# A scan kernel on one Trainium2 core: the product with C in two halves, each behind a scan of other columns

## The chip, the core and the metric

The kernel runs on one core of a Trainium2 chip. The metric is the device time of one execution in microseconds (us); the time of the kernel before is the median of three runs. The engines are named as in the profile: PE (matrix products), DVE (vector), ACT (activations), POOL (general elementwise), SP (which issues most DMAs). SBUF is the on-chip memory; PSUM is the small memory that PE writes its results to.

## The reference

Two layers on an image `x` of shape 4 x 512 x 64 x 64, both with a residual. The first cuts the 512 channels in four chunks of 128 and runs a Mamba block on each; the second is a linear attention. The heart of the first layer, and of the time, is a recurrence over 4096 positions for 256 inner channels and 16 states:

```python
def step(h, inp):
    dt_t, B_t, C_t, x_t = inp
    dA = jnp.exp(dt_t[:, :, None] * A)
    h = dA * h + (dt_t * x_t)[:, :, None] * B_t[:, None, :]
    y = jnp.einsum('bds,bs->bd', h, C_t)
    return (h, y)
...
y = ys.transpose(1, 0, 2) + xc * D_param
y = y * jax.nn.silu(z)
return jnp.einsum('bld,od->blo', y, out_proj_w)
```

Around it stand a group norm, a layer norm, the input and output projections, a second layer norm and a projection; then the attention layer with its own group norm. The change concerns the line `y = einsum(h, C_t)`: the product of every state with C, and the sum over states.

## The kernel before

**Tiling.** The positions are cut in 8 tiles of 512. A *step* is one batch, one tile and one of the four chunks: 4 x 8 x 4 = 128 steps. In a step the 256 inner channels (2 halves) times 16 states make 32 rows of 128 partitions: a partition holds one of 32 channels with one of 4 states. These rows are taken in *groups* of four scans; 8 groups make a step, 1024 groups the loop. The code counts in *slots* of two scans: 16 slots a step, 2048 in all; `jj` is 0 for a group's first slot and 1 for its second.

**A group.** For each scan ACT computes `dA` (`decay`, L713) into one of three PSUM buffers, three scans ahead. POOL computes `bx` for two scans at once (`drive`, L721), two slots ahead, into one of three buffers. DVE runs `tensor_tensor_scan` (L739) into `h[:, j, :]`, one quarter of the tile `h` (128 x 4 x 512); `h` has two buffers. After the fourth scan the whole of `h` is multiplied by C: POOL takes the last 128 of the 512 positions (L750, with C in SBUF, behind a copy of the last column to the state `st`, L749), DVE the first 384 (L754, `CUT` is 384), with C in PSUM: `c_all`, one buffer, written by PE (`c_row`) out of the step's row of C.

**The sum over states.** `fold_states` (L757) runs one scan into the next group: PE writes the next group's `c_all` (which has to wait until the product has read the last one), at a half's first group it starts the accumulator `y` with D times x (`diagonal`), and then adds the group's `h` into `y` by eight matmuls with `fold`. The first scan of the group after the next overwrites this `h`, so it waits for these.

**The order of the work.** The order on each engine is that of the program (a manual schedule). `slot` issues the two scans with their `decay`, then the products, then calls `after`, which hands out everything else by slot number: convolution and projections of the step after next on PE (`pc`, `pz`, `pd`), softplus of the next step at slot 3 with its table loads on ACT (`time_steps`, L620), silu at slot 10 (L1044), the copy of `y` out of PSUM at slots 0 and 8 (`take_y`, L774), the gate and the output projection of the step before, layer norms, and the attention of the batch before in the gaps (`pq`, `pk`, `pr`). PE, ACT, POOL and DVE each take their instructions strictly in this order: one that waits holds up all behind it on its engine.

In this document a group's *place* is its number in its step, 0 to 7; place p covers slots 2p and 2p + 1.

Of the kernel before, what the change touches and what calls it, by code (L numbers as in the profile page):

```python
# [11 lines left out]
ALU = mybir.AluOpType  # L12
# [12 lines left out]
def kernel(  # L25
# [24 lines left out]
    nc = tc.nc  # L50
# [7 lines left out]
    CUT = T - T // 4  # L58
# [3 lines left out]
    NJ = P // BLK  # L62
# [58 lines left out]
    def mm(out_, lhsT, rhs, abreast=1, **how):  # L121

        work["mm"] += (0.25 if rhs.dtype == BF16 else 1.0) * rhs.shape[-1] / T / abreast
        nc.tensor.matmul(out_, lhsT, rhs, **how)  # L124
# [3 lines left out]
    def diagonal(out_, w, rhs):  # L128

        for k in range(P // BLK):  # L130
            r = slice(k * BLK, (k + 1) * BLK)
            mm(out_[r, :], w[r, :], rhs[r, :], abreast=P // BLK, start=True, stop=False)
# [242 lines left out]
    def bc(v, n):  # L375
        return v.unsqueeze(1).to_broadcast([P, n, v.shape[-1]])
# [296 lines left out]
    JJ = NJ // 2  # L673
    SLOTS = NH * NQ * JJ
    AWAY = (3, 10)

    def place(g):

        n, r = divmod(g, SLOTS)
        e, r = divmod(r, NQ * JJ)  # L680
        return n, e, *divmod(r, JJ)

    b_all, c_all, c_sb, dAs, bxs, hs, ys = {}, {}, {}, {}, {}, {}, {}
# [8 lines left out]
    def b_row(g):  # L692
        n, e, q, _ = place(g)
        b_all[g // JJ] = wk.tile([P, T], F32, tag="b_all", name=f"b_all_{g}", bufs=3)
        for_states(b_all[g // JJ], fs[n]["b_rows"], q)

    def c_tail(g):
        n, e, q, _ = place(g)
        c_sb[g // JJ] = wk.tile([P, T - CUT], F32, tag="c_sb", name=f"c_sb_{g}", bufs=2)
        for_states(c_sb[g // JJ], fs[n]["c_rows"], q)  # L700

    def c_row(g):
        n, e, q, _ = place(g)
        got = ps_c.tile([P, CUT], F32, tag="c", name=f"c_all_{g}")
        mm(got, sel[:, q, :], fs[n]["parts"], start=True, stop=True)
        c_all[g // JJ] = got

    def decay(k):

        n, e, q, jj = place(k // 2)  # L710
        j = jj * 2 + k % 2
        dAs[k] = ps_d.tile([P, T], F32, tag="dA", name=f"dA_{k}")
        nc.scalar.activation(  # L713
            dAs[k], fs[n]["d_all", e][:, 0, j, :], AF.Exp, scale=a_t[:, e, j, q : q + 1]
        )

    def drive(g):

        n, e, q, jj = place(g)
        bxs[g] = wk.tile([P, 2, T], F32, tag="bx", name=f"bx_{g}", bufs=3)  # L720
        nc.gpsimd.tensor_tensor(  # L721
            bxs[g], fs[n]["d_all", e][:, 1, jj * 2 : jj * 2 + 2, :], bc(b_all[g // JJ], 2), ALU.mult
        )

    def slot(g, last, after):
        n, e, q, jj = place(g)
        b, t, c = steps[n]
        if g + 2 < last:
            drive(g + 2)
        if jj == 0:  # L730
            if g + 3 * JJ < last:
                b_row(g + 3 * JJ)
            hs[g // JJ] = wk.tile([P, NJ, T], F32, tag="h", name=f"h_{g}", bufs=2)
        elif g + 1 < last:
            c_tail(g + 1)
        h = hs[g // JJ]
        for i in range(2):
            j = jj * 2 + i
            nc.vector.tensor_tensor_scan(  # L739
                h[:, j, :], dAs.pop(2 * g + i), bxs[g][:, i, :],  # L740
                0.0 if t == 0 else st[:, c, e, q, j : j + 1], ALU.mult, ALU.add,
            )
            if 2 * g + i + LEAD < 2 * last:
                decay(2 * g + i + LEAD)
            if i == 0 and jj == 0 and g:
                fold_states(g - 1, last)
        del bxs[g]
        if jj == JJ - 1:
            nc.gpsimd.tensor_copy(st[:, c, e, q, :], h[:, :, T - 1])  # L749
            nc.gpsimd.tensor_tensor(  # L750
                h[:, :, CUT:], h[:, :, CUT:], bc(c_sb.pop(g // JJ), NJ), ALU.mult
            )
            own = h[:, :, :CUT]
            nc.vector.tensor_tensor(own, own, bc(c_all.pop(g // JJ), NJ), ALU.mult)  # L754
        after()

    def fold_states(g, last):  # L757

        n, e, q, _ = place(g)
        if g + 1 < last:  # L760
            c_row(g + 1)
        if q == 0:
            ys[n, e] = ps_y.tile([P, T], F32, tag="y", name=f"y_{n}_{e}")
            diagonal(ys[n, e], dg[:, e, :], fs[n]["xz"][:, 0, e, :])
        h = hs.pop(g // JJ)
        for j in range(NJ):
            mm(
                ys[n, e][j * BLK : (j + 1) * BLK, :], fold, h[:, j, :],
                start=False, stop=(q == NQ - 1), abreast=NJ,
            )  # L770
# [232 lines left out]
    N = len(steps)  # L1003
# [86 lines left out]
    with tc.manual_schedule():  # L1090
        credit, seen, mix, held[0], held_x[0] = 0.0, work["mm"], iter(()), 0, 0
        for n, (b, t, c) in enumerate(steps):
# [10 lines left out]
            for s in range(SLOTS):  # L1103
                def after():
# [62 lines left out]
                    seen = work["mm"]  # L1167

                slot(n * SLOTS + s, N * SLOTS, after)
            fs[n - 1].clear() if n else None  # L1170
        fold_states(N * SLOTS - 1, N * SLOTS)
        now[0] = None
        for _, what in due:
# [61 lines left out]
```

## Time and profile before

| what | value |
|---|---|
| median of three runs | 8033.95 us (8033.66 to 8039.26) |
| the profiled execution | 8026.47 us, of it the span shown in the profile 8024.7 us |
| loop, from the first product to the last | about 128 to 7558 us |
| end of the attention, after the loop | about 465 us |
| DVE's scans | 4096, mean 1.20 us with a constant start value (512 of them), 1.27 us otherwise |
| DVE's product with C | 1024, mean 1.755 us |
| POOL's product with C | 1024, mean 1.272 us |
| POOL's `bx` | 2048, mean 2.367 us |
| ACT's `dA` | 4096, mean 0.687 us |

Every time in the profile is from one profiled execution. A group's row gives the number of instructions, their busy time, the mean of one, and the idle time of the engine just before them with what ended it. Busy shares are means over the whole span, the start and the end of the attention included; the time of a change to the loop is read from the loop. Instructions of DVE may overlap a little at their ends, so that the sum of their durations is more than the time they take.

### The profile page before, as it was taken

Reading aid. Unit: us, or ns where it says so; the run is one execution under the profiler, and the core shown is the slowest. Engines: PE = TensorE matmul, PEld = TensorE weight load, DVE = VectorE, ACT = ScalarE, POOL = GpSimd, SP = SyncE. Lnnn points to the kernel's source line nnn. Section 1 sums busy time; section 2 is a strip of 40 time slices with the busy share of each in tenths; the row PEclk is TensorE's granted clock in tenths of the full one; section 3 lists DMA queues with packets and bytes.
Section 4 is the critical chain, followed back from the end, with each engine's and each line's share of the span. In section 5 each row is a group of like instructions: output and inputs, shape, how many; then the busy total and the mean of one; then the engine's idle time right before and its main releaser. Section 6 shows DMA issues by size and latency. Waiting matters only on the chain.

```text
span 8024.7 us, 91633 instructions
## 1 busy us (share of the span) xinstructions
PE 6503.6 (81%) x24880; PEld 2132.3 (27%) x24880; DVE 7050.9 (88%) x5766; ACT 5545.6 (69%) x8321; POOL 6886.8 (86%) x4597
## 2 busy tenths in 40 slices
PE   5676777677788888888788888888788888888599
PEld 1121211121223222322222222322122232322144
DVE  5999999999999999989999999999999999998600
ACT  4667777777777777777777777777777777776421
POOL 4999999999999899889999989899999989889600
PEclk7888888887899999999899999999899999999799
DMA  5666666666666666676666656677666666677402
GB/s 157 165 166 162 149 148 158 156 158 158 172 164 167 151 163 155 172 192 169 171 159 169 174 151 159 160 182 189 158 164 158 157 154 157 156 186 185 116 32 89
DMA packets 829192, 1265.93 MB, mean 158 GB/s; under 512 B 183912, under 2 KB 317560, under 8 KB 816384
## 3 DMA queue, kind: packets, MB, share of 16 engines
q1 hardware_dynamic: 804736, 1222.32, 59.9%
q0 software_dynamic: 16896, 33.56, 2.4%
q10 hardware_dynamic: 7040, 4.20, 0.2%
q8 instruction: 195, 3.19, 0.2%
q14 instruction: 325, 2.66, 0.1%
HBM read 1052.78 MB, written 206.57 MB: 157 GB/s over the span
## 4 chain that ended last, share of the span: by engine, by line
PE 29%; DVE 27%; ACT 22%; issue 8%; DMA 6%; POOL 3%; SPq 2%; DVEq 0%; POOLq 0%; ACTq 0%
DVE h L739 24%; ACT dA L713 9%; PE pc L124 8%; PE pq L124 5%; PE y L124 4%; DMA d_all<-d_rows 3%; PE po L124 3%; PE pp L124 3%; PE pr L124 3%; ACT xz L1044 2%; POOL bx L721 2%; SPq L688 2%; ACT L1145 1%; ACT L1044 1%; ACT L1123 1%
## 5 line engine op out<-in xcount | busy, mean ns | idle before, releaser
L721 POOL TENSOR_TENSOR bx<-d_all,b_all 128x1024 f32<-128x1024 f32 x2048 | 4827.4, 2367 | 283.6 <-DVE h L739 268.0
L739 DVE TENSOR_TENSOR_SCAN h<-dA,st,bx 128x512 f32<-128x512 f32 x3584 | 4330.9, 1265 | 207.7 <-ACT dA L713 196.3
L713 ACT ACTIVATE dA<-d_all,a_t 128x512 f32<-128x512 f32 x4096 | 2756.8, 687 | 1539.7 <-DVE h L739 1506.1
L754 DVE TENSOR_TENSOR h<-h,c_all 128x1536 f32<-128x1536 f32 x1024 | 1796.9, 1755 | 189.8 <-PE c_all L124 88.9
L750 POOL TENSOR_TENSOR h<-h,c_sb 128x512 f32<-128x512 f32 x1024 | 1302.2, 1272 | 153.5 <-DMA c_sb<-c_rows 56.1
L124 PE MATMUL y<-h,fold 128*32 128x512 f32 x8192 | 1251.1, 686 | 124.3 <-POOL h L750 119.7
L124 PE MATMUL pc<-xn,w_cv 128*128 128x512 f32 x2048 | 1107.0, 677 | 255.8 <-ACT dt L620 156.8
L124 PE MATMUL c_all<-parts,sel 128*128 128x384 bf16 x1024 | 359.5, 351 | 875.2 <-DVE h L754 873.6
L124 PE MATMUL pq<-w_qk,xa 128*128 128x512 f32 x2048 | 968.8, 606 | 2.2 <-ACT xa L367 2.2
L739 DVE TENSOR_TENSOR_SCAN h<-dA,bx 128x512 f32<-128x512 f32 x512 | 587.6, 1204 | 68.6 <-ACT dA L713 67.8
L124 PEld LDWEIGHTS pc<-xn,w_cv 128*128 128x128 f32 x2048 | 405.4, 209 | 899.6 <-issue 424.1
L124 PEld LDWEIGHTS pq<-w_qk,xa 128*128 128x128 f32 x2048 | 400.1, 197 | 494.5 <-issue 478.7
L124 PEld LDWEIGHTS y<-h,fold 128*32 128x32 f32 x8192 | 169.4, 113 | 1349.5 <-POOL h L750 866.1
L124 PE MATMUL pr<-xb,m 128*128 128x512 f32 x1024 | 488.9, 616 | 15.9 <-DMA xb<-x 11.9
L124 PE MATMUL pp<-xn,w_pr 128*128 128x512 f32 x1024 | 477.4, 597 | 6.0 <-DVE xn L414 6.0
L828 ACT ACTIVATE kq<-pq 128x512 f32<-128x512 f32 x256 | 150.4, 587 | 270.5 <-PE pq L124 269.9
L777 POOL TENSOR_TENSOR xz<-xz 128x512 f32<-128x512 f32 x256 | 325.0, 1270 | 11.7 <-ACT xz L774 7.8
L124 PE MATMUL y<-xz,dg 32*32 32x512 f32 x2048 | 333.4, 726 | 0.0
L628 POOL TENSOR_TENSOR dt<-dt,xz 128x1024 f32<-128x1024 f32 x128 | 302.0, 2359 | 22.6 <-ACT dt L620 22.6
L124 PE MATMUL pd<-xz,w_xp 128*128 128x512 f32 x512 | 314.4, 745 | 7.8 <-ACT xz L1044 7.8
L749 POOL COPY st<-h 128x4 f32<-128x4 f32 x1024 | 210.2, 205 | 108.3 <-DVE h L739 91.2
L124 PE MATMUL pz<-xn,w_z 128*128 128x512 f32 x512 | 273.9, 627 | 8.8 <-DVE kq L835 3.3
(179 smaller groups left out, 5991.5 us busy)
## 6 DMA issues: line engine op xcount, KB each, us to landing
d_all<-d_rows SPq DMA_DIRECT2D x2048, 256.0 KB, 6.5
b_all<-b_rows SPq DMA_DIRECT2D x4096, 64.0 KB, 2.1
d_rows<-dt SPq DMA_DIRECT2D x256, 512.0 KB, 3.7
c_sb<-c_rows SPq DMA_DIRECT2D x4096, 16.0 KB, 1.8
xs<-in_x_dram SPq DMA_DIRECT2D x32, 1024.0 KB, 5.8
xn<-in_x_dram SPq DMA_DIRECT2D x32, 1024.0 KB, 5.8
xr<-in_x_dram POOLq DMA_DIRECT2D x32, 1024.0 KB, 10.5
x<-xr SPq DMA_DIRECT2D x32, 1024.0 KB, 4.2
```

Of the source, the lines that this page charges most:

```text
L124: nc.tensor.matmul(out_, lhsT, rhs, **how)
L628: nc.gpsimd.tensor_tensor(f["both"][:, 1], f["both"][:, 0], f["xz"][:, 0], ALU.mult)
L688: nc.sync.dma_start(dst[k * BLK : (k + 1) * BLK, :], rows_[q * KS + k, :].partition_broadcast(BLK))
L713: nc.scalar.activation(dAs[k], fs[n]["d_all", e][:, 0, j, :], AF.Exp, scale=a_t[:, e, j, q : q + 1])
L721: nc.gpsimd.tensor_tensor(bxs[g], fs[n]["d_all", e][:, 1, jj * 2 : jj * 2 + 2, :], bc(b_all[g // JJ], 2), ALU.mult)
L739: nc.vector.tensor_tensor_scan(h[:, j, :], dAs.pop(2 * g + i), bxs[g][:, i, :], 0.0 if t == 0 else st[:, c, e, q, j : j + 1], ALU.mult, AL ...
L749: nc.gpsimd.tensor_copy(st[:, c, e, q, :], h[:, :, T - 1])
L750: nc.gpsimd.tensor_tensor(h[:, :, CUT:], h[:, :, CUT:], bc(c_sb.pop(g // JJ), NJ), ALU.mult)
L754: nc.vector.tensor_tensor(own, own, bc(c_all.pop(g // JJ), NJ), ALU.mult)
L777: nc.gpsimd.tensor_tensor(f["xz"][:, 1, e, :], f["xz"][:, 1, e, :], f["xz"][:, 0, e, :], ALU.mult)
L828: nc.scalar.activation(qk[i], pq, AF.Relu)
L1044: nc.scalar.activation(fs[n]["xz"], fs[n]["xz"], AF.Silu)
```

## The change

The product with C on DVE is cut in two halves of two scans each. The first half, columns of the scans `j` = 0 and 1, stands where the whole product stood, behind the group's fourth scan. The second half, `j` = 2 and 3, is issued in the next group's first slot, behind its first scan and ahead of `fold_states`. In the order of DVE:

```
before: scan 0, scan 1, scan 2, scan 3, product(0..3) | scan 0, scan 1, ...
after:  scan 0, scan 1, scan 2, scan 3, product(0, 1) | scan 0, product(2, 3), scan 1, ...
```

`c_all` is no longer taken out of its table by the product, since both halves read it. The last group's second half follows the loop. The order on PE, ACT, POOL and SP is the same as before. On PE the wait for the product with C, which stood on the matmul that writes the next `c_all`, stands on the weight load ahead of it, and waits for the second half.

```diff
             if 2 * g + i + LEAD < 2 * last:
                 decay(2 * g + i + LEAD)
             if i == 0 and jj == 0 and g:
+                product(g - 1, 1)
                 fold_states(g - 1, last)
         del bxs[g]
         if jj == JJ - 1:
...
             nc.gpsimd.tensor_tensor(
                 h[:, :, CUT:], h[:, :, CUT:], bc(c_sb.pop(g // JJ), NJ), ALU.mult
             )
-            own = h[:, :, :CUT]
-            nc.vector.tensor_tensor(own, own, bc(c_all.pop(g // JJ), NJ), ALU.mult)
+            product(g, 0)
         after()
+
+    def product(g, jj):
+
+        own = hs[g // JJ][:, jj * 2 : jj * 2 + 2, :CUT]
+        nc.vector.tensor_tensor(own, own, bc(c_all[g // JJ], 2), ALU.mult)
...
             fs[n - 1].clear() if n else None
+        product(N * SLOTS - 1, 1)
         fold_states(N * SLOTS - 1, N * SLOTS)
```

## The prediction

> **What bounds the kernel now.** I read the busy shares first, then the same engines by stretch, then who waits for whom, then DVE's own timeline. Shares of the whole span and the three costliest groups:
>
> ```profile
> PE 6503.6 (81%) x24880; PEld 2132.3 (27%) x24880; DVE 7050.9 (88%) x5766; ACT 5545.6 (69%) x8321; POOL 6886.8 (86%) x4597
> L721 POOL TENSOR_TENSOR bx<-d_all,b_all 128x1024 f32<-128x1024 f32 x2048 | 4827.4, 2367 | 283.6 <-DVE h L739 268.0
> L739 DVE TENSOR_TENSOR_SCAN h<-dA,st,bx 128x512 f32<-128x512 f32 x3584 | 4330.9, 1265 | 207.7 <-ACT dA L713 196.3
> L754 DVE TENSOR_TENSOR h<-h,c_all 128x1536 f32<-128x1536 f32 x1024 | 1796.9, 1755 | 189.8 <-PE c_all L124 88.9
> ```
>
> Busy time by stretch (us, then PE, PEld, DVE, ACT, POOL):
>
> ```profile
> 2000.00:4000.00 2000.00, 1683.56 (x6549) 554.32 (x6550) 1874.01 (x1523) 1470.78 (x2215) 1837.06 (x1225) 0.92 0.67 167
> 4000.00:6000.00 2000.00, 1687.79 (x6621) 559.97 (x6620) 1872.67 (x1526) 1473.21 (x2217) 1833.55 (x1223) 0.92 0.66 167
> 7560.00:8024.00 464.00, 429.27 (x1510) 195.57 (x1508) 22.99 (x72) 103.85 (x167) 4.14 (x4) 0.95 0.18 59
> ```
>
> Inside the loop DVE is busy 94% of the time and POOL 92%; PE 84%, ACT 74%. The last 464 us are PE's alone, and the change doesn't touch them. DVE's timeline (start, us, what; merged):
>
> ```profile
> 2562.20 1.76 DVE L754 TENSOR_TENSOR h<-h,c_all 128x1536 f32<-128x1536 f32 x1
> 2563.88 4.80 DVE L739 TENSOR_TENSOR_SCAN h<-dA,st,bx 128x512 f32<-128x512 f32 x4
> 2568.78 1.75 DVE L754 TENSOR_TENSOR h<-h,c_all 128x1536 f32<-128x1536 f32 x1
> ```
>
> Two things stand here. Four scans of 1.26 us take 4.80 and not 5.04: each begins about 0.084 before the one ahead ends, and so does the scan behind a product (2563.88, though 2562.20 + 1.76 = 2563.96). Only the product does not: the scans end at 2568.68 and it starts at 2568.78, because it reads what the last scan wrote and waits for it. From product to product: 6.58 us. Who waits (us in total, times, longest):
>
> ```profile
> DVE h L739 <- ACT dA L713: 264.1, 175, 46.7
> DVE h L754 <- PE c_all L124: 88.9, 76, 3.0
> DVE h L739 <- POOL bx L721: 4.3, 6, 1.7
> PE c_all L124 <- DVE h L754: 873.6, 356, 9.1
> PE pc L124 <- ACT dt L620: 156.8, 67, 4.1
> ```
>
> So 1024 x 6.58 = 6738 of the loop's 7430 us are the chain of scans and products, some 350 are DVE's norms and sums, and some 340 (after the first product) are waits for others. DVE sets the pace, in places relieved by ACT and PE.
>
> [...]
>
> **The change part by part.**
> 1. The wait. In the built program the first half waits for DVE's second scan of the group (two scans behind it), the second half for the fourth scan, with a half product and a scan between. So both waits are over before their turn comes. Scan-to-product falls from 1.365 (1.26 + 0.105) to 1.175 (1.26 - 0.084): -0.19 us a group.
> 2. One more instruction. Short products of the same kind are in the trace: L835, 256 elements, takes 0.399 behind a scan and 0.417 behind a product; the norm's subtraction (L428), 2048 elements, 2.262 behind a scan. Slope (2.262 - 0.399)/1792 = 1.04 ns an element, so 768 elements behind a scan: 0.399 + 512 x 0.00104 = 0.931; less the overlap, 0.847. Two of them 1.694, against 1.672 for the whole one. [...] A scan behind a product takes 1.277 and not 1.259, and there are now two of those: +0.018.
> 3. Sum of a group: 2 x 0.847 + 2 x 1.193 + 2 x 1.175 = 6.43 against 6.58: -0.15 us [...]. Over 1024 groups 154 us [...]: the ceiling.
> 4. What of it reaches the end. Sorting the trace by group, 268 of 1024 product-to-product intervals hold a wait of DVE for another engine. They cluster: in a step of 8 groups (place 0 to 7), place 6 (94 waits for ACT, behind silu and its table loads) and place 2 to 4 (73 for ACT, 69 for c_all). ACT's interludes start behind a scan and last as long as before, so there the wait grows by what the group saves: no gain. Before a late c_all the groups from place 2 on gain nothing either; with those, 358 groups are lost and 666 gain: 666 x 0.15 = 100 us.
> 5. PE is released later. With the fourth scan's start as zero, the product ended at 1.365 + 1.755 = 3.12; the second half ends at 1.175 + 0.847 + 1.193 + 0.931 = 4.15. c_all of the next group, its weight load (which now holds the wait, 0.10) and the y products come 1.03 to 1.13 us later, and c_all is needed 0.34 earlier (0.19 + 0.15). Where PE had waited for the product, 4.4 us were left between c_all and the next product; 3 remain. Where PE comes late (place 2 to 5), the release isn't what it waits for: between c_all of place 1 and of place 2 it stood idle for ACT's dt (softplus), median 2.0 us, and dt hangs on a scan, not on the product. That idle time hides the 1.1 us; it is shorter than 1.1 in 45 of 126 steps, and only some of these have a tight c_all behind them: sum of shortfalls 12 us. In the 65 steps with a c_all that comes within 0.2 us of its product, the 0.19 already won at place 1 is lost too: 12 us.
> 6. h has two buffers, and a group's first scan waits for the y products of two groups before. y ends 1.00 us behind c_all. Before, a product of 1.67 covered that; now a half of 0.85 does. Where c_all is late, that adds some 0.17 us: 95 times, 16 us. The 24 at place 5 (y behind another matmul, 1.99) are covered by ACT's wait at place 6.
> 7. ACT, POOL and SP keep their order, and all DMAs theirs. ACT reads y one us later, but reaches that copy only behind the next group's second scan. POOL's tail product (L750) touches other columns and waits for the same scan. In 6 steps of about 53.5 us POOL is busy from end to end: 6 x 1 us are not to be had.
> Sum: 100 - 12 - 12 - 16 - 6 = 54 us. On the profiled execution: span 8024.7 to 7971 (8026.5 with what lies around it to 7973). The median of the runs is 7.5 above that execution: 8034 to 7980.
>
> **The rivals.**
> - *The whole ceiling.* The waiters are themselves driven by scans; if ACT's and PE's waits shrink with the more even rhythm (the fourth scan's dA gets 0.85 us more cover), nearly all arrives: 8034 - 154 = 7880. Against it: the ACT interludes of about 4.5 us at place 6 don't shrink.
> - *Absorbed.* POOL, 92% busy, or PE takes over as the bound: about 8025, from 8015 to 8034. For it: POOL's load is 2% below DVE's. Against it: POOL's bx lead its scans by a median of 3 to 5 us, and DVE waited for them 4.3 us in all.
> - *PE's lag decides (slower).* Place: c_all and y behind the second half. If PE's late stretch in each step hangs on the release and not on dt, every step loses 1.1 us: 128 x 1.1 = 141, less 100 gained, plus the 34 of points 6, 7 and the lost 0.19: +75, 8109. The point from which it decides is PE's idle time before the step's first pc falling to nothing; if it holds in three quarters of the steps, it is +40: 8074.
> - *It doesn't do what it says.* Were the first half still held till the last scan, only the costs remained: +0.04 us a group and points 5 and 6, about 8100. The waits of the built program speak against it.
>
> **How the numbers follow.** Likeliest 0.52 (its own range 7945 to 8010), ceiling 0.15, absorbed 0.15, PE's lag 0.14, not as said 0.04. A measurement here tells 0.2% (16 us) from no change. Faster: 0.51 + 0.15 + a third of the absorbed, 0.71. Same: 0.11. Slower: 0.14 + 0.04, 0.18. The range for 8 in 10 goes down to 7905, [...] and up to 8045, which takes in the absorbed case and the mild end of PE's lag.
>
> **What would show it.** Right: gap between the fourth scan and the first half -0.08 us and not +0.10; halves of 0.93; undisturbed groups of 6.43; DVE's waits for ACT up by 10 to 30 us; PE's wait for DVE before c_all about as long as before, moved into the weight load. Wrong: halves over 1.0, first scans waiting for y in hundreds of places, PE's wait for dt gone and DVE's for c_all doubled.

## The result, and the profile after

| | median, us | runs | ratio to before, 95% interval |
|---|---|---|---|
| before | 8033.8 | 4, 8031.7 to 8039.3 | |
| after | 7992.2 | 4, 7985.9 to 7998.0 | 0.9947 (0.9930 to 0.9964) |
| after, once more with later experiments | 7994.2 | 5, 7986.1 to 7996.0 | 0.9943 (0.9931 to 0.9956) |

The change takes 42 us off (8033.8 - 7992.2), forecast were 54. The profiled execution went from 8026.5 to 7990.5, its span from 8024.7 to 7988.8. The page of the changed kernel, the rows of DVE's loop and of PE's `c_all`:

```profile
PE 6502.1 (81%) x24835; PEld 2128.4 (27%) x24880; DVE 7037.6 (88%) x6790; ACT 5528.9 (69%) x8321; POOL 6881.1 (86%) x4597
L739 DVE TENSOR_TENSOR_SCAN h<-dA,st,bx 128x512 f32<-128x512 f32 x3584 | 4411.6, 1266 | 265.7 <-ACT dA L713 199.8
L760 DVE TENSOR_TENSOR h<-h,c_all 128x768 f32<-128x768 f32 x2048 | 1897.2, 926 | 92.7 <-PE c_all L124 92.4
L124 PE MATMUL c_all<-parts,sel 128*128 128x384 bf16 x1024 | 369.4, 361 | 1073.3 <-DVE h L760 1071.8
```

A half takes 0.926 us. The idle time ahead of the product on DVE, 189.8 us before, is 92.7, and nearly all of that is now the wait for `c_all` (92.4): the 0.1 us that stood in front of each product is gone. The scans' busy time is larger (4411.6 us for 4330.9) though one takes as long as before (1.266 for 1.265): busy time counts an overlap within a group of the page once, and the scans now overlap halves where they overlapped each other. DVE's timeline of the changed kernel (start, us, what; equal neighbours merged):

```profile
2559.02 0.93 DVE L760 TENSOR_TENSOR h<-h,c_all 128x768 f32<-128x768 f32 x1
2559.86 1.27 DVE L739 TENSOR_TENSOR_SCAN h<-dA,st,bx 128x512 f32<-128x512 f32 x1
2561.06 0.93 DVE L760 TENSOR_TENSOR h<-h,c_all 128x768 f32<-128x768 f32 x1
2561.91 3.62 DVE L739 TENSOR_TENSOR_SCAN h<-dA,st,bx 128x512 f32<-128x512 f32 x3
2565.45 0.93 DVE L760 TENSOR_TENSOR h<-h,c_all 128x768 f32<-128x768 f32 x1
```

From first half to first half: 6.43 us, where a group took 6.58. The first half at 2565.45 begins before the scans end (2561.91 + 3.62 = 2565.53); in this stretch every instruction overlaps the one ahead. Who waits (us in total, times, longest):

```profile
DVE h L739 <- ACT dA L713: 268.0, 192, 46.7
DVE h L760 <- PE c_all L124: 92.4, 67, 2.6
DVE h L739 <- PE y L124: 36.6, 69, 1.2
DVE h L739 <- POOL bx L721: 25.6, 23, 4.0
PE c_all L124 <- DVE h L760: 1071.8, 430, 10.1
PE pc L124 <- ACT dt L620: 78.1, 53, 2.9
```

What is new: scans that wait for `y` (36.6 us, 3.1 before) and for `bx` (25.6, 4.3 before). PE waits longer for the product (873.6 before) and less for dt (156.8 before), as it would if the later release moves PE's idle time from one place to the other.

Sorted by place, the interval from one group's fourth scan to the next one's, mean in us (worked out from the traces; the interval ends at the place named):

| place | 0 | 1 | 2 | 3 | 4 | 5 | 6 | 7 |
|---|---|---|---|---|---|---|---|---|
| before | 6.70 | 6.60 | 8.52 | 6.93 | 7.18 | 7.60 | 7.86 | 6.71 |
| after | 6.58 | 6.47 | 8.56 | 6.88 | 7.35 | 7.50 | 7.85 | 6.62 |

Places 7, 0, 1 and 5 gain about 0.1 a group, place 3 half of that. Places 2 and 6 gain nothing, as forecast: there ACT's softplus (3.86 us with its two table loads of 1.28 us each) and silu (4.51 us with its two) stand ahead of `dA`, and DVE waits for `dA` 93.6 and 96.3 us, of 268.0 in all. Place 4 loses 0.17: there the waits for a late `c_all` (65 us in all, 50 before, the overlap lost by the wait counted in) and most of those for `bx` (17 us of 29) come together.

### The profile page after: what moved, and what is told of

The parts are those of the page before. It is cut to its first block, busy times and chain, and to the rows that moved or that the text cites. A ratio compares the mean times of both kernels' runs of the same rounds, so it can differ in the third digit from the quotient of the medians.

```text
span 7988.8 us, 92611 instructions
## 1 busy us (share of the span) xinstructions
PE 6502.1 (81%) x24835; PEld 2128.4 (27%) x24880; DVE 7037.6 (88%) x6790; ACT 5528.9 (69%) x8321; POOL 6881.1 (86%) x4597
## 4 chain that ended last, share of the span: by engine, by line
PE 30%; DVE 27%; ACT 17%; DMA 10%; issue 8%; SPq 4%; POOL 3%; DVEq 0%; POOLq 0%; ACTq 0%
DVE h L739 17%; DVE h L760 8%; PE pc L124 7%; ACT dA L713 7%; PE pq L124 5%; PE y L124 5%; DMA d_all<-d_rows 5%; SPq L688 3%; PE pp L124 3%; PE pr L124 2%; PE po L124 2%; POOL bx L721 2%; ACT xz L1049 2%; DMA c_sb<-c_rows 1%; SPq L639 1%
## 5 line engine op out<-in xcount | busy, mean ns | idle before, releaser
L739 DVE TENSOR_TENSOR_SCAN h<-dA,st,bx 128x512 f32<-128x512 f32 x3584 | 4411.6, 1266 | 265.7 <-ACT dA L713 199.8
L760 DVE TENSOR_TENSOR h<-h,c_all 128x768 f32<-128x768 f32 x2048 | 1897.2, 926 | 92.7 <-PE c_all L124 92.4
L124 PE MATMUL y<-h,fold 128*32 128x512 f32 x8192 | 1276.0, 699 | 84.9 <-POOL h L751 84.1
L124 PE MATMUL c_all<-parts,sel 128*128 128x384 bf16 x1024 | 369.4, 361 | 1073.3 <-DVE h L760 1071.8
L124 PE MATMUL pc<-xn,w_cv 128*128 128x512 f32 x2048 | 1084.9, 665 | 150.3 <-ACT dt L620 78.1
L124 PEld LDWEIGHTS <-sel 128*128 128x128 bf16 x1280 | 127.5, 100 | 1712.1 <-DVE h L760 1466.0
```

The costliest lines, as they stand in the source:

```text
L739: nc.vector.tensor_tensor_scan(h[:, j, :], dAs.pop(2 * g + i), bxs[g][:, i, :], 0.0 if t == 0 else st[:, c, e, q, j : j + 1], ALU.mult, AL ...
L760: nc.vector.tensor_tensor(own, own, bc(c_all[g // JJ], 2), ALU.mult)
```

## The experiments

The theory: each undisturbed group gains 0.15 us because the product no longer waits for the scan ahead; where another engine is late the gain is lost, and the later release of PE takes some more. The rivals: POOL or ACT absorb what DVE saves; the gain has another source than the wait. All ratios are to the kernel before on the same chip.

**Both halves behind the fourth scan** (the split without the move):

```diff
             if i == 0 and jj == 0 and g:
-                product(g - 1, 1)
                 fold_states(g - 1, last)
...
             product(g, 0)
+            product(g, 1)
```

> Both halves stand behind the fourth scan, the second half straight behind the first; nothing is moved past the next group's first scan. Theory (the 0.15 us of each undisturbed group comes from the wait that goes; what is lost on the way is the later release of PE, seen as first scans that wait for y and products that wait for c_all): an undisturbed group again takes 6.43 us (1.175 + 0.847 + 0.865 + 1.193 + 2 x 1.175), DVE's waits for y fall from 36.6 us to under 10, PE's release comes 0.15 us before that of the kernel before, and the time is 7930 to 7955. Rival (the rest of the gain is taken by POOL and by ACT's interludes, wherever the half stands): 7980 to 8000, as with the changed kernel. Rival (the distance of a scan is needed, an adjacent half still waits): groups of 6.6 us and 8030 or more.

Measured: 7972.8 us, ratio 0.9924 (0.9911 to 0.9938); an undisturbed group takes 6.43 us. DVE's waits in that kernel:

```profile
DVE h L739 <- ACT dA L713: 306.2, 195, 46.4
DVE h L760 <- PE c_all L124: 102.0, 82, 3.9
DVE h L739 <- POOL bx L721: 19.2, 23, 2.8
DVE h L739 <- PE y L124: 4.4, 15, 0.3
```

The waits for `y` are nearly gone, as expected, and the time is 19 us below the changed kernel's (7992.2 - 7972.8). It isn't as low as I put it: with `y` on time, DVE waits 38 us more for ACT and 10 more for `c_all` than in the changed kernel. So these four kinds of wait don't say where the 19 us lie: together they are 432 us here and 423 in the changed kernel. By place, it is place 4 that shrinks, from 7.35 to 7.21 us (18 us in 128 steps).

DVE's timeline of this kernel shows both halves starting without a gap:

```profile
2549.74 4.80 DVE L739 TENSOR_TENSOR_SCAN h<-dA,st,bx 128x512 f32<-128x512 f32 x4
2554.46 1.79 DVE L760 TENSOR_TENSOR h<-h,c_all 128x768 f32<-128x768 f32 x2
```

The halves start at 2554.46, before the scans end (2554.54), and overlap each other. The second half needs no scan between itself and what it reads; the first half is distance enough. So the split by itself brings the gain, and the kernel that also moves the second half past the next group's first scan is 19 us slower.

One thing beside the order differs. These runs had a granted PE clock of 0.894 to 0.896, those of the changed kernel 0.888 to 0.892, and among the runs of one kernel those at a higher clock tend to be shorter (two further down, at 0.892, took 7974 and 7977 us; one of the same kernel at 0.888 took 8004). Whether PE's order sets that clock, and how much of the 19 us goes with it, was not tested. The same holds for the two kernels below that move the whole product (0.896 to 0.899).

**The split with the wait kept**: as above, but the half that reads the third and fourth scan first.

```diff
-            product(g, 0)
             product(g, 1)
+            product(g, 0)
```

> Both halves behind the fourth scan, the half that reads the third and fourth scan first: the split alone, with the wait for the last scan kept. Theory: an undisturbed group takes 6.65 us (0.07 more than before: two halves of 0.87 net for one product of 1.67), 8060 to 8085. Rival (the gain came from shorter instructions or from the split, not from the wait): below 8020.

Measured: 8074.3 us, ratio 1.0049 (1.0035 to 1.0063). Its DVE timeline:

```profile
2557.72 4.80 DVE L739 TENSOR_TENSOR_SCAN h<-dA,st,bx 128x512 f32<-128x512 f32 x4
2562.63 1.82 DVE L760 TENSOR_TENSOR h<-h,c_all 128x768 f32<-128x768 f32 x2
2564.37 2.45 DVE L739 TENSOR_TENSOR_SCAN h<-dA,st,bx 128x512 f32<-128x512 f32 x2
```

The scans end at 2562.52 and the halves start at 2562.63: the gap of 0.1 us is back, and group to group takes 2564.37 - 2557.72 = 6.65 us. This kernel and the pair have the same instructions and differ in the order of two of them; 0.22 us a group (6.65 - 6.43) and 101 us in all (8074.3 - 7972.8) lie between. That settles the source: it is the wait for the scan ahead.

**The product whole, behind the next group's first scan** (the move without the split):

```diff
             if i == 0 and jj == 0 and g:
-                product(g - 1, 1)
+                product(g - 1)
...
-            product(g, 0)
...
-        own = hs[g // JJ][:, jj * 2 : jj * 2 + 2, :CUT]
-        nc.vector.tensor_tensor(own, own, bc(c_all[g // JJ], 2), ALU.mult)
+        own = hs[g // JJ][:, :, :CUT]
+        nc.vector.tensor_tensor(own, own, bc(c_all[g // JJ], NJ), ALU.mult)
```

> The product whole, one instruction, behind the next group's first scan: the wait goes without a split. Theory: an undisturbed group takes 6.36 us (0.22 less than before), but the first scan of a group now stands ahead of the product and needs the y products of two groups before, so that DVE's waits for PE y rise to 60 to 150 us; 7940 to 8000. Rival (POOL or ACT is the bound once DVE saves anything): 7985 to 8000 with more waits for dA and bx instead of y.

Measured: 7964.7 us, ratio 0.9911 (0.9897 to 0.9924); an undisturbed group takes 6.365 us. The waits that stand out:

```profile
DVE h L739 <- ACT dA L713: 225.3, 183, 46.7
DVE h L739 <- PE y L124: 84.5, 81, 3.7
DVE h L739 <- POOL bx L721: 84.2, 74, 4.6
```

One instruction less a group, and the wait hidden too; paid for with scans that wait for `y`, as expected, and with as much for `bx`, which I had left to the rival. Both are right in part; the time is in the theory's range, and 28 us below the changed kernel (7992.2 - 7964.7).

**The second half and the sum one scan later**:

```diff
-            if i == 0 and jj == 0 and g:
+            if i == 1 and jj == 0 and g:
                 product(g - 1, 1)
                 fold_states(g - 1, last)
```

> As the changed kernel, but the second half and the sum over states stand one scan later, behind the next group's second scan: PE's release another 1.2 us later, DVE's instructions the same. Theory (the later release is what costs): waits of DVE for c_all and y rise by 30 to 80 us together, 8015 to 8060. Rival (the release is hidden and POOL and ACT take the rest): within 0.2% of the changed kernel, 7976 to 8008.

Measured: 8094.9 us, ratio 1.0072 (1.0058 to 1.0086): slower than before, though an undisturbed group still takes 6.43 us. The waits of this kernel, DVE's first, then PE's, then ACT's:

```profile
DVE h L739 <- ACT dA L713: 339.3, 230, 46.6
DVE h L760 <- PE c_all L124: 60.7, 56, 3.1
DVE h L739 <- PE y L124: 57.9, 80, 1.4
PE pc L124 <- ACT dt L620: 41.8, 40, 1.7
ACT xz L779 <- PE y L124: 345.4, 241, 7.4
```

The direction is the theory's, the time is above its range, and the road is another: waits for `c_all` and `y` together fell (118.6 for 129.0). What rose is ACT's: its copy of `y` out of PSUM waits 345 us for PE, 127.4 in the changed kernel, and the `dA` behind it come late (339 for 268). By place, the interval at 2 grows to 8.90 us, at 6 to 8.16, at 7 to 6.97. PE's idle time ahead of `pc` falls again. So the later release is cheap for one scan and dear for two: in the changed kernel ACT reaches that copy behind the next group's second scan and waits for `y` hardly longer than before (127.4 us, 124.7 before). That the late copy is what delays the `dA` is read from the waits and not tested; and DVE's waits for ACT, `c_all`, `y` and `bx` together rose by 57 us, of the 109 between the two spans (8097.4 and 7988.8).

**y before D times x**: in a half's first group PE adds the group's `h` first.

```diff
         for j in range(NJ):
             mm(
                 ys[n, e][j * BLK : (j + 1) * BLK, :], fold, h[:, j, :],
-                start=False, stop=(q == NQ - 1), abreast=NJ,
+                start=(q == 0), stop=(q == NQ - 1), abreast=NJ,
             )
+        if q == 0:
+            diagonal(ys[n, e], dg[:, e, :], fs[n]["xz"][:, 0, e, :], False)
```

> As the changed kernel, but in a half's first group PE adds the group's h into y first and D times x (1.0 us) behind it, so that h is free 1.0 us sooner twice a step. Theory (the first scan at place 6 waits for y because that matmul stands ahead, and ACT's wait covers only part of it): DVE's waits for PE y fall from 36.6 us to 5 to 15, the time falls by 8 to 25 us: 7967 to 7984. Rival (ACT's wait at place 6 takes over in full): waits for dA rise by as much, 7986 to 7998.

Measured: 7990.0 us (7974 to 8004, 6 runs), ratio 0.9940 (0.9928 to 0.9951): the changed kernel's time. Its waits:

```profile
DVE h L739 <- ACT dA L713: 305.5, 194, 48.2
DVE h L739 <- PE y L124: 7.2, 36, 0.8
```

29 us of waits for `y` go, 38 of waits for `dA` come: at place 6, where 29.5 of the 36.6 us were, DVE now waits for ACT's silu instead (31 us more), so a wait removed there shows the one beneath. The median is in the rival's range too. But the runs lie far apart: the profiled one, at 7976.5, and one at 7974 are in the theory's range, the other four are not. A gain of some us is not excluded.

**POOL relieved**: POOL's product with C for two of the four scans only, on the changed kernel and on the kernel before.

```diff
             nc.gpsimd.tensor_tensor(
-                h[:, :, CUT:], h[:, :, CUT:], bc(c_sb.pop(g // JJ), NJ), ALU.mult
+                h[:, :2, CUT:], h[:, :2, CUT:], bc(c_sb.pop(g // JJ), 2), ALU.mult
             )
```

> As the changed kernel, but POOL's product with C is done for the first two of the four scans only (0.63 us less on POOL a group; the last 128 positions of the other two are left without C). Theory (POOL takes a small part of the gain): DVE's waits for bx fall from 25.6 us to near 0, 7955 to 7975. Rival (POOL is the bound that absorbed the gain): 7930 or less, towards the ceiling of 7880.

> The kernel before with the same cut of POOL's product (the last 128 positions of the third and fourth scan are left without C): what POOL costs there. Theory: 10 to 15 us less than before, 8018 to 8030, so that POOL took 10 to 20 us more from the changed kernel. Rival (POOL costs both the same): the changed kernel and this one fall by the same amount.

Measured: 7967.3 us on the changed kernel, ratio 0.9915 (0.9902 to 0.9928), 8040.4 on the one before, 1.0004 (0.9995 to 1.0012). Before, POOL costs nothing, not even the 10 us of my expectation; after, the relief is worth 25 to 27 us (7992.2 or 7994.2 less 7967.3). Three of DVE's waits in the relieved changed kernel:

```profile
DVE h L739 <- PE y L124: 20.4, 54, 1.2
DVE h L739 <- POOL h L751: 18.3, 22, 1.2
DVE h L739 <- POOL bx L721: 15.4, 10, 3.1
```

Waits for `bx` don't go to nothing (15.4 of 25.6 stay), against the theory. Those for `y` fall by 16 us, but those for POOL's own product with C rise by as much (18.3, 1.3 in the changed kernel), nearly all at place 6: one stands in for the other. The profiled run, at 7979.1, is the slowest of the four and only 11 us shorter than the profiled one of the changed kernel, so its waits can't show the whole 25 us. By place it is again place 4 that shrinks, from 7.35 to 7.22 us (17 us in 128 steps). The clock was 0.889 to 0.890, as in the changed kernel. So it is shown that POOL, which cost nothing before, takes a share once DVE is faster; by which wait is shown only in part. It isn't the bound that takes all, or the time had gone to 7930.

**Both together**: both halves behind the fourth scan, and POOL relieved in the same way.

> Both halves behind the fourth scan, and POOL's product with C done for the first two scans only (the last 128 positions of the other two are left without C). Theory (PE's later release and POOL each took their own part of the gain, 20 and 25 us): the two add up, 7940 to 7955. Rival (they are the same loss, seen once as a wait for y and once as one for bx): no better than the better of the two alone, 7963 to 7975.

Measured: 7954.4 us (7952 to 7965, 4 runs), ratio 0.9901 (0.9885 to 0.9916); the changed kernel beside it 7994.2 (the last row of the first table). For that one this was expected:

> The changed kernel once more, beside the next one on the same chip, as the base of comparison. Expected 7984 to 8000.

Alone, the two were worth 19 and 25 us; together 40 (7994.2 - 7954.4), 18 below the pair alone and 13 below the relief alone. They nearly add up: two losses, for the most part, and not one seen twice. There is no trace of this kernel. What would fit is a wait of the pair's: PE waits 239.9 us there for POOL's product with C ahead of `y`, where it waits 84.1 in the changed kernel and 29.2 in the relieved one.

**A faster order**: the whole product behind the next group's first scan, and PE does `y`, then the next `c_all`, then D times x.

```diff
-        if g + 1 < last:
-            c_row(g + 1)
         if q == 0:
             ys[n, e] = ps_y.tile([P, T], F32, tag="y", name=f"y_{n}_{e}")
-            diagonal(ys[n, e], dg[:, e, :], fs[n]["xz"][:, 0, e, :])
...
+        if g + 1 < last:
+            c_row(g + 1)
+        if q == 0:
+            diagonal(ys[n, e], dg[:, e, :], fs[n]["xz"][:, 0, e, :], False)
```

> The product whole behind the next group's first scan, and in the sum over states PE does y first, then the next c_all (which is now needed a scan later), then D times x. Theory (the waits for y are what is left of the moved product's gain): DVE's waits for y fall from 84.5 us to 20 to 50, 7920 to 7955, faster than both kernels and than both halves behind the fourth scan (7973). Rival (POOL is the next bound): waits for bx rise from 84 us to 110 or more and the time stays within 10 us of 7965.

Measured: 7949.0 us, ratio 0.9889 (0.9876 to 0.9902): faster than both kernels, and than the product moved alone (7964.7). The time is in the range I gave, but by luck, for its waits say that the reason is not the one I gave:

```profile
DVE h L739 <- ACT dA L713: 296.2, 203, 46.7
DVE h L739 <- PE y L124: 83.0, 74, 3.7
DVE h L739 <- POOL bx L721: 51.4, 48, 4.4
```

The waits for `y` stayed (83.0 for 84.5); those for `bx` fell (51.4 for 84.2) and those for `dA` rose (296.2 for 225.3). The rival, more waits for `bx`, is wrong as well. Why PE's order shortens the waits for POOL, and what the 16 us come from, was not tried and stays open.

## Why the prediction was right

The sum was 100 gained, 46 lost, 54 in all; 42 were measured. The gain was right in cause and size; that the losses come out so near is in part luck, since one term was too small and others too large.

- *The wait and the second instruction (points 1 to 3).* Right to the hundredth: gap -0.08, halves 0.926 (0.931 forecast), groups 6.43. The second half ends 4.14 us behind the fourth scan's start (4.15 forecast). The reversed pair shows that the wait is the source, and that the split alone costs 0.07 us a group.
- *What reaches the end (point 4).* 666 groups of 0.15 were to give 100 us. In the traces some 685 of 1023 intervals hold no wait in either kernel, and together they are some 99 us shorter (0.144 each). Places 2 and 6 gained nothing, as said. What shrank the 99 to some 37 in the loop lies in the other 340 intervals or so.
- *The later release and the two buffers (points 5 and 6).* 12 + 16 us were put down for them; putting the second half back behind the first is worth 19. The 16 were too many: first scans wait 36.6 us for `y`, but 29.5 of these at place 6, where waits for ACT take their place when they go, as forecast, and only 7 elsewhere. The idle time behind dt shrank (156.8 to 78.1), as it must if it covers the later release; that it covered most of it is argued, not shown.
- *POOL (point 7).* The term that was mis-sized most. I counted 6 us, from 6 steps in which POOL works from end to end; relieving it gives 25 to 27 in the changed kernel, 18 in the pair, and nothing in the kernel before. A reading at fault: that `bx` leads its scans by a median of 3 to 5 us. The low end of that lead is what counted here. In the kernel before it is shortest at places 3 and 4; at place 4's first scan the median is 4.0 us, yet a tenth of the leads are below about 1.4. In the changed kernel a tenth of them there are below 0.05, and 15.6 of the 25.6 us of waits for `bx` are at this place. These waits are only a part of what POOL takes. With 25 us in place of 6 the sum would have been 35, and with 19 in place of 12 + 16 as well, 44.
- *The slower rival* (PE's lag decides) didn't happen, but one scan later the kernel is slower than before, 8095. By its waits it goes another way than I wrote, over ACT's copy of `y`, and not over `c_all`.
- *The ceiling* (7880) was not reached: ACT's waits didn't shrink (268.0 us for 264.1). The low end of my range, 7905, was an estimate that no run shows.
- *The signs.* Two of those named for a right forecast did not come: DVE's waits for ACT rose by 4 us (264.1 to 268.0) and not by 10 to 30, and PE's wait for DVE before `c_all` rose by 198 (873.6 to 1071.8) and did not stay. The signs named for a wrong one did not come either: 69 waits for `y`, not hundreds; half of PE's wait for dt left; DVE's wait for `c_all` at 92.4 for 88.9.

## What to carry to other kernels

An instruction on DVE that reads what the one straight ahead of it wrote paid for the wait here, 0.19 us each time, though both are on one engine. Look for the gap between the two in the timeline, multiply it by the count, and let something that doesn't read it stand between, a piece of the same instruction if nothing else is there. If the whole instruction can go behind an independent one, try that first: uncut it took 7964.7 us here, in two pieces 7972.8 at best. Order the pieces so that the one that reads the last result comes last (7972.8 us here, and 8074.3 the other way round), and don't move it further than the distance needs, since others wait for its end (moved behind one scan it took 7992.2, behind two 8094.9). When DVE's groups got faster by 2% here (6.43 us for 6.58), POOL, busy for 92% of the loop where DVE was for 94%, cost 25 to 27 us, and nothing before: read the lead of the engine next behind at the low end, not at the median. And when one wait goes, add up all of them: here others rose, and the sum of the waits often did not tell where the time went.

## What the runs showed of the hardware

- A scan or a product that had no wait overlapped the instruction ahead by about 0.08 us (mostly 0.084 in the kernel before, 0.08 in the changed one). A product with a wait for the scan just ahead started 0.105 us behind its end instead (median of 1024 in the kernel before). One instruction of 0.93 us between was enough to make the wait free: in the pair the second half overlaps the first by 0.08.
- The duration of the product in the trace differed with what was ahead. A half of 768 elements took 0.925 us (median) behind a scan without a wait, 0.946 behind the other half in the pair, and 0.954 or 0.955 after a wait. The whole product of 1536 elements took 1.755 us after the wait for the scan ahead, and 1.728 where it is moved behind the next group's first scan.
- A wait held up what stood behind it on its engine. In the kernel before, ACT's copy of `y` (L774) waits for PE 102 times, 124.7 us in all. In 78 of these a `dA` comes next; in 76 of the 78 the scan that frees its buffer had ended more than 0.3 us before the copy began, and the `dA` still started behind the copy. ACT's 8321 instructions and POOL's 4597 start in the same order in the traces of both kernels.
